# A two-layer graph kernel: which share of the source rows is copied as table columns by ScalarE and VectorE, and which is gathered by GpSimd

## The chip, the cores and the metric

The kernel runs on one core of a Trainium2 chip. Its time is the device time of one execution in microseconds (us). Three runs took 4564.47 us in the median, 4559.45 at the lowest and 4566.27 at the highest. One further execution was profiled. The engines are called as the profile calls them: PE (TensorE, with PEld for its weight loads), DVE (VectorE), ACT (ScalarE), POOL (GpSimd) and SP (SyncE, which only issues DMAs here).

## The reference, cut to what matters

The graph has N = 12500 nodes with 128 features each, and E = 200000 edges, sorted by destination. Two message-passing layers are computed.

```
h     = max(layernorm(x), 0)
feat  = relu(h @ W_pool + b_pool)
neigh = segment_max(feat[src] * w, dst)             # layer 1: a maximum per node
h1    = relu(normalize(h @ W1_self + neigh @ W1_neigh + b1))
agg   = segment_sum(h1[src] * w, dst) / deg         # layer 2: a sum per node
out   = x + relu(h1 @ W2_self + agg @ W2_neigh + b2)
```

What costs time is the reading of `feat[src]` and `h1[src]`: for each of the 200000 edges, and in each layer, one row of 128 floats at a place that only the data knows.

## The kernel before

**Groups and chunks.** The edges are taken in 391 groups of 512, and a group in four chunks of 128 edges (the last group has three chunks). A chunk's source rows land as a tile of 128 edges by 128 features in a buffer of the group. A chunk is filled in one of two ways.

**A gather** is one indirect DMA that POOL issues (`gather`, L581): 128 rows of 512 bytes are read from the table in DRAM (`feat_d` in layer 1, `h_d` in layer 2). POOL does nothing else in the main loops but issue gathers and wait for buffers.

**A column chunk** (class `Columns`) doesn't touch DRAM for its rows. Beside the table in DRAM there is a transposed table in SBUF (`one_way` in layer 1, `other_way` in layer 2), in which a node is one column over 128 partitions. The list of a chunk's 128 column addresses is loaded by SP (`load`), read 16 at a time into registers (`places_of`, L803), and then ACT copies one column per instruction (`one_by_one`, L849) or DVE two columns per instruction (`two_by_two`, L865). That makes 128 ACT or 64 DVE instructions for a chunk. Eight bursts of 16 columns (`fetch`) are planned over the turns before the group is due. After them the chunk has to be turned: in layer 1 by a product with the weights (`multiplied`, L1019 and L1020) and an ACT pass (`cut`, L1023), in layer 2 by a transpose on PE (`turned`, L1213) and an ACT copy back (`back`).

**Which groups.** `every` and `first` say which groups have a column chunk. In layer 1 DVE has one in each 6th group from group 32 on, ACT one in each 5.5th from 28 on. In layer 2 DVE has one in each 3rd from 17 on, ACT one in each 3.5th from 12 on. That is 126 column chunks in layer 1 and 228 in layer 2. `gather` leaves out the chunk that a `Columns` object takes.

**Turns.** Each layer is one Python loop whose turns are written out in order; each engine runs its instructions in that order. In layer 1, turn i issues the gathers of group i, transposes group i on PE (`pm`, L1102), scans group i-1 on DVE with the running maximum (L1117), picks, transposes and places the results of the groups before (`sc`, `pr` L1157, `rows` L1112, `pn` L1166, window copy L1051), and now and then finishes a tile of nodes (`nodes1`). In layer 2, turn i issues the gathers of group i, makes the group's weighted place matrix on DVE (`place` L1227, `s` L1231), multiplies group i-1 on PE (`pa`, L1239), and adds the product of group i-2 to the sums on DVE (L1242).

**How far POOL runs ahead.** POOL's queue holds gathers alone, so POOL is ahead of the other engines until a buffer is missing. In layer 1 the number of buffers falls as the sums fill the memory they are lent from: 38 up to group 75, then 20, 16, 12 and 8 (`ROOM`, `ring_at`). In layer 2 there are 16. `follow` adds waits: from group 60 on in layer 1, and in all of layer 2, a gather of group i also waits for what `mark` noted in an earlier turn (i minus `lag_of(i)`, or i minus 10): PE's transposes in layer 1, and in both layers each eighth ACT column copy of that turn.

```
made = nc.gpsimd.indirect_dma_start(out=gt[:k, j, :], ...)
if behind is not None:
    follow(made, g - behind, n / len(left))
```

The functions that the diff touches, and what calls them, with the line numbers of the profile:

Of the kernel before, what the change touches and what calls it, by code (L numbers as in the profile page):

```python
# [45 lines left out]
CATCH = 9  # L46
# [9 lines left out]
def gnn_kernel(ctx, tc, x, src, dst, ew, w_pool, b_pool, w1s, w1n, b1, w2s, w2n, b2, out):  # L56
# [14 lines left out]
    N = x.shape[0]  # L71
# [5 lines left out]
    NG = GF + 1  # L77
# [587 lines left out]
    for i in range(len(groups) + 4):  # L665
# [59 lines left out]
        while raw_chunks and i <= 15:  # L725
            r, j = raw_chunks[0]
# [8 lines left out]
        k = i - len(groups)  # L735
# [33 lines left out]

    class Columns:  # L770

        def __init__(self, engine, copy, ahead_of, table, layer, lists, slot, after, lead, j, every, first, end):
            self.engine, self.copy, self.ahead_of = engine, copy, ahead_of
            self.table, self.layer, self.at = table.bitcast(U8), layer, TABLES_AT[layer]
            self.lists, self.slot, self.j = lists, slot, j
            self.place, self.held, self.plan = {}, {}, {}
            self.order, self.ready, self.pending = [], set(), None
            while (g := first + int(len(self.place) * every)) < end:
                self.place[g] = len(self.place) % 2
                begin = g - int(every) - lead  # L780
                steps = P // BURST
                assert begin >= 3
                for turn, step in ((begin - 2, self.load), *((g + k, step) for k, step in after)):
                    self.plan.setdefault(turn, []).append((step, g, 0))
                for k in range(steps):
                    turn = begin + int(k * every / steps)
                    self.plan.setdefault(turn, []).append((self.fetch, g, k * BURST))
                    self.order.append((g, k * BURST, turn))

# [55 lines left out]
    def lists_of(k):  # L845
        return [listed[at:at + 1, :] for at in (64 * k, 64 * k + 32)]

    def by_scalar(out, in_, **scale):
        return nc.scalar.activation(out, in_, AF.Copy, **scale)  # L849
# [141 lines left out]
    with tc.manual_schedule(), tc.tile_pool(name="ew", bufs=3) as wk, \  # L991
# [12 lines left out]
        pms, scs, sels, prs, rws, pas = ({} for _ in range(6))  # L1004
        products = {}
        bycol = []
        for k, engine, copy, j, every, first in (
                (0, mybir.EngineType.DVE, two_by_two, 1, 6, 32),
                (1, mybir.EngineType.Activation, one_by_one, 3, 5.5, 28)):
# [12 lines left out]
            def cut(g, _, k=k, rows_of_chunk=rows_of_chunk):  # L1022
                nc.scalar.activation(rows_of_chunk(g), products.pop((g, k)), AF.Relu,  # L1023
                                     **({} if k else {"scale": signs}))

            bycol.append(Columns(engine, copy, k == 0, one_way, 0, lists_of(k), slot,
                                 ((-2, multiplied), (-1, cut)), 2, j, every, first, NG - 1))
            bycol[k].multiplied, bycol[k].cut = multiplied, cut
        turn = turns(wide1, 6)
        busy = {}  # L1030
# [11 lines left out]
        def due(k):  # L1042

            return i - k if 0 <= i - k < NG else None
# [24 lines left out]
        end = NG - 1  # L1069
        for i in range(max(turn) + 6):  # L1070
# [35 lines left out]
            g = due(3)  # L1106
# [6 lines left out]
            g = due(1)  # L1113
# [38 lines left out]
            g = due(2)  # L1152
# [7 lines left out]
            g = due(4)  # L1160
# [33 lines left out]
    with tc.manual_schedule(), tc.tile_pool(name="ew2", bufs=3) as wk, \  # L1194
# [7 lines left out]
        nc.vector.memset(nothing, 0.0)  # L1202

        bycol = []
        for k, engine, copy, j, every, first in (
                (0, mybir.EngineType.DVE, two_by_two, 1, 3, 17),
                (1, mybir.EngineType.Activation, one_by_one, 2, 3.5, 12)):

            def slot(g, j=j):
                return buffer(g, False)[:, j, :]  # L1210

            def turned(g, _, k=k, slot=slot):
                nc.tensor.transpose(flip[:, k], slot(g), ident)  # L1213

            def back(g, _, k=k, slot=slot):
                by_scalar(slot(g), flip[:, k], **({} if k else {"scale": signs}))

            bycol.append(Columns(engine, copy, None, other_way, 1, lists_of(k), slot,
                                 ((-2, turned), (0, back)), 3, j, every, first, NG - CATCH))
# [55 lines left out]
        turn = turns(wide2, 3, 2 * EARLY * (Q + 6))  # L1275
# [3 lines left out]
        for i in range(max(turn) + 2):  # L1279
# [19 lines left out]
            g = i - 1  # L1299
# [10 lines left out]
            g = i - 2  # L1310
# [29 lines left out]
    with tc.If(flag > 0):  # L1340
        with tc.tile_pool(name="gt", bufs=1) as tp, tc.tile_pool(name="gw", bufs=2) as wk, \
# [79 lines left out]
def build(inputs):  # L1421
    import numpy as np
    import concourse.bacc as bacc

    nc = bacc.Bacc("TRN2", target_bir_lowering=False, num_devices=1)
    arrays, args = {}, []
    for name in _INS:
        a = np.ascontiguousarray(inputs[name])
        arrays[f"in_{name}"] = a
        args.append(nc.dram_tensor(f"in_{name}", a.shape, mybir.dt.from_np(a.dtype),  # L1430
                                   kind="ExternalInput").ap())
    args.append(nc.dram_tensor("out", inputs["x"].shape, F32, kind="ExternalOutput").ap())
    with tile.TileContext(nc) as tc:
        gnn_kernel(tc, *args)
    return nc, arrays
# [7 lines left out]
```

## Time and profile before

| | us |
|---|---|
| median of three runs | 4564.47 |
| the profiled execution, its own time | 4560.5 |
| its span, first to last instruction | 4558.6 |
| busy PE / PEld | 2224.7 / 1911.2 |
| busy DVE | 3150.7 |
| busy ACT | 2829.6 |
| busy POOL | 2620.6 |

Busy is the time in which an engine had an instruction in execution; the shares of the span are an average over a preparation (up to about 160 us), layer 1 (up to about 2370 us) and layer 2. A row of the groups reads: line, engine, operation, what is written from what, shape, count, then busy us, the mean ns of one, and the idle time just before them with what ended it. "issue" means that the profile shows nothing that the engine waited for, "remote" a semaphore whose sender the profile doesn't name. A row of the windows gives, for a stretch of the span, each engine's busy us and in brackets its number of instructions.

### The profile page before, as it was taken

What the parts mean: (1) busy time and instruction counts of PE and PEld (TensorE: products, weight loads), DVE (VectorE), ACT (ScalarE), POOL (GpSimd) and SP (SyncE); (2) the same over time, 40 slices, a digit from 0 to 9 for tenths busy, and PEclk for the clock granted to TensorE, in tenths of its full rate; (3) what the DMA queues carried; (4) which work ended last, traced back from release to release, by engine and by line L of the source; (5) the groups of instructions that cost most, each with busy time, mean ns of one, the idle gap of its engine ahead of it and who ended that gap; (6) DMA issues with size and microseconds to landing.
All of it is one profiled execution on the core that took longest, in us unless ns stands there. A gap on an engine that the chain in (4) does not pass through costs nothing.

```text
span 4558.6 us, 71416 instructions
## 1 busy us (share of the span) xinstructions
PE 2224.7 (49%) x9505; PEld 1911.2 (42%) x9505; DVE 3150.7 (69%) x16224; ACT 2829.6 (62%) x23893; POOL 2620.6 (57%) x2789
## 2 busy tenths in 40 slices
PE   5525654545555555554443545444444444444445
PEld 3314544444444444444442444344334434434444
DVE  4437987778878777877772667666666666666663
ACT  3425755566666655655543777777777777777773
POOL 5556266665665666566656555555555555555554
PEclk7555555555555555555555555555555555555555
DMA  5313233332332323333321112111111111111111
GB/s 159 101 54 103 77 98 95 96 93 93 96 93 91 96 88 95 92 94 95 94 83 44 41 44 57 48 46 48 49 45 48 47 48 46 48 49 47 49 49 41
DMA packets 136652, 328.01 MB, mean 72 GB/s; under 512 B 50865, under 2 KB 59538, under 8 KB 136164
## 3 DMA queue, kind: packets, MB, share of 16 engines
q0 software_dynamic: 88704, 181.75, 15.7%
q1 hardware_dynamic: 45652, 140.69, 8.6%
q14 instruction: 408, 3.34, 0.2%
q8 instruction: 80, 1.31, 0.1%
q10 hardware_dynamic: 1808, 0.92, 0.1%
HBM read 300.80 MB, written 22.39 MB: 71 GB/s over the span
## 4 chain that ended last, share of the span: by engine, by line
ACT 51%; issue 27%; PE 7%; another core or an unknown queue 5%; DVE 4%; ACTq 4%; DMA 0%; DVEq 0%; POOL 0%; POOLq 0%; SPq 0%
ACT gt L849 25%; ACT ewT L849 7%; ACT way L849 5%; ACTq L803 4%; ACT lastT L849 4%; ACT invT L849 4%; ACT rows L1112 1%; PE pn L1166 1%; PE pr L1157 1%; ACT way L1051 1%; PE pa L1239 1%; DVE pm L1117 1%; PE pf L682 1%; PE pm L1102 1%
## 5 line engine op out<-in xcount | busy, mean ns | idle before, releaser
L849 ACT ACTIVATE gt<-way 128x1 f32 x12032 | 1309.0, 190 | 633.4 <-issue 620.3
L581 POOL DMA_INDIRECT gt<-feat_d,srcT x777 | 733.2, 944 | 570.9 <-issue 176.6
L581 POOL DMA_INDIRECT gt<-h_d,srcT x669 | 631.8, 944 | 449.8 <-issue 122.5
L1157 PE MATMUL pr<-ident,sc 128*128 128x128 f32 x782 | 257.6, 432 | 1025.2 <-ACT rows L1112 635.9
L581 POOL DMA_INDIRECT way<-feat_d,srcT x547 | 517.4, 946 | 338.4 <-issue 122.6
L865 DVE SCALAR_TENSOR_TENSOR gt<-b,way 128x2 f32<-128x2 f32 x3968 | 572.3, 217 | 129.0 <-issue 119.9
L1117 DVE TENSOR_TENSOR_SCAN pm<-kt,pm 128x512 f32<-128x512 f32 x389 | 500.6, 1287 | 153.5 <-remote 91.7
L1157 PEld LDWEIGHTS pr<-ident,sc 128*128 128x128 f32 x782 | 125.5, 206 | 1127.0 <-ACT rows L1112 693.5
L1239 PE MATMUL pa<-s,gt 128*128 128x24 f32 x1566 | 384.0, 390 | 393.6 <-ACT gt L849 223.3
L865 DVE SCALAR_TENSOR_TENSOR picked<-b,way 128x2 f32<-128x2 f32 x3840 | 542.9, 217 | 14.7 <-issue 13.8
L1239 PEld LDWEIGHTS pa<-s,gt 128*128 128x128 f32 x1566 | 353.3, 325 | 423.1 <-ACT gt L849 228.0
L849 ACT ACTIVATE ewT<-way 128x1 f32 x3456 | 370.2, 189 | 139.9 <-issue 136.5
L581 POOL DMA_INDIRECT ewT<-h_d,srcT x327 | 308.5, 943 | 220.4 <-ACT gt L849 108.6
L849 ACT ACTIVATE way<-way 128x1 f32 x2816 | 311.7, 193 | 187.7 <-issue 185.9
L1166 PEld LDWEIGHTS pn<-sel,rows 128*128 128x128 f32 x1564 | 369.8, 325 | 15.7 <-DVE r L934 8.9
L1242 DVE TENSOR_TENSOR way<-pa,way 128x48 f32 x391 | 80.0, 205 | 410.7 <-PE pa L1239 191.0
L1166 PE MATMUL pn<-sel,rows 128*128 128x48 f32 x1564 | 355.3, 375 | 9.8 <-DVE r L934 7.6
L865 DVE SCALAR_TENSOR_TENSOR ewT<-b,way 128x2 f32<-128x2 f32 x1920 | 276.7, 217 | 65.5 <-issue 62.4
L1139 DVE COPY sc<-pm 128x256 f32<-128x256 f32 x391 | 165.3, 423 | 224.3 <-PE pr L1157 113.4
L849 ACT ACTIVATE lastT<-way 128x1 f32 x1920 | 208.0, 189 | 133.0 <-issue 131.2
L1239 PE MATMUL pa<-s,ewT 128*128 128x24 f32 x768 | 188.6, 390 | 204.0 <-ACT ewT L849 104.0
L1239 PEld LDWEIGHTS pa<-s,ewT 128*128 128x128 f32 x768 | 173.5, 325 | 228.5 <-ACT ewT L849 106.2
(352 smaller groups left out, 5032.5 us busy)
## 6 DMA issues: line engine op xcount, KB each, us to landing
kt<-ratio_d SPq DMA_DIRECT2D x129, 768.0 KB
gt<-feat_d,srcT POOLq DMA_INDIRECT x777
gt<-h_d,srcT POOLq DMA_INDIRECT x669
way<-feat_d,srcT POOLq DMA_INDIRECT x547
feat_d<-fr SPq DMA_DIRECT2D x24, 256.0 KB
xr<-in_x SPq DMA_DIRECT2D x24, 256.0 KB
out<-o SPq DMA_DIRECT2D x24, 256.0 KB
h_d<-h SPq DMA_DIRECT2D x47, 128.0 KB
```

The lines of the kernel that those rows point to most:

```text
L581: made = nc.gpsimd.indirect_dma_start(out=gt[:k, j, :], out_offset=None, in_=table_d[:, :], in_offset=bass.IndirectOffsetOnAxis(ap=places, ...
L682: nc.tensor.matmul(pf[:, q, :], rows[:, q, :], W["pool"], start=False, stop=q == n - 1)
L803: _, self.held[g, r] = nc.values_load_multi_w_load_instructions(self.lists[self.place[g]][:, r:r + BURST], [self.engine], min_val=self.at, ...
L849: return nc.scalar.activation(out, in_, AF.Copy, **scale)
L865: nc.vector.scalar_tensor_tensor(slot[:, r + e:r + e + 2], zero_high, columns_read[e], columns_read[e + 1].to_broadcast([P, 2]), op0=OP.su ...
L1051: nc.scalar.activation(agg1[:, bass.ds(at, LW)], pas.pop(g), AF.Copy)
L1117: nc.vector.tensor_tensor_scan(pm[:, :ne], kt[:, :ne], pm[:, :ne], carry, op0=OP.mult, op1=OP.max)
L1139: nc.vector.tensor_copy(sc[:, :ne // 2], two[:, :, 0])
L1157: nc.tensor.transpose(prs[g][:k, j, :], sc[:, j * P:j * P + k], ident)
L1166: nc.tensor.matmul(pas[g], rows[:k, j, :], sel[:k, j, :], start=j == 0, stop=j == len(chunks) - 1)
L1239: nc.tensor.matmul(pas[g][:, SHIFT[j]:SHIFT[j] + CW], gt[:k, j, :], s[:k, j, :], start=False, stop=j == 0)
L1242: nc.vector.tensor_tensor(agg2[:, bass.ds(at, LW)], pas.pop(g), agg2[:, bass.ds(at, LW)], OP.add)
```

## The change

`Columns` gets one more parameter, `spread`: the turns over which the eight bursts of a chunk are laid out, which was `every` so far. In layer 1 the first group of both `Columns` objects becomes N = 12500, which lies beyond the last group, so that no chunk of layer 1 is a column chunk. In layer 2 DVE has one in each 14th group from 22 on and ACT one in each 13th from 20 on, that is 26 and 28 chunks, with their bursts spread over 11 turns. A gather by POOL takes the place of each column chunk that is gone: 126 in layer 1 and 174 in layer 2.

```diff
-        def __init__(self, engine, copy, ahead_of, table, layer, lists, slot, after, lead, j, every, first, end):
+        def __init__(self, engine, copy, ahead_of, table, layer, lists, slot, after, lead, j, every, spread, first, end):
...
             while (g := first + int(len(self.place) * every)) < end:
                 self.place[g] = len(self.place) % 2
-                begin = g - int(every) - lead
+                begin = g - int(spread) - lead
...
                 for k in range(steps):
-                    turn = begin + int(k * every / steps)
+                    turn = begin + int(k * spread / steps)
...
-                (0, mybir.EngineType.DVE, two_by_two, 1, 6, 32),
-                (1, mybir.EngineType.Activation, one_by_one, 3, 5.5, 28)):
+                (0, mybir.EngineType.DVE, two_by_two, 1, 6, 6, N),
+                (1, mybir.EngineType.Activation, one_by_one, 3, 5.5, 5.5, N)):
...
-                                 ((-2, multiplied), (-1, cut)), 2, j, every, first, NG - 1))
+                                 ((-2, multiplied), (-1, cut)), 2, j, every, spread, first, NG - 1))
...
-                (0, mybir.EngineType.DVE, two_by_two, 1, 3, 17),
-                (1, mybir.EngineType.Activation, one_by_one, 2, 3.5, 12)):
+                (0, mybir.EngineType.DVE, two_by_two, 1, 14, 11, 22),
+                (1, mybir.EngineType.Activation, one_by_one, 2, 13, 11, 20)):
...
-                                 ((-2, turned), (0, back)), 3, j, every, first, NG - CATCH))
+                                 ((-2, turned), (0, back)), 3, j, every, spread, first, NG - CATCH))
```

More of the change, by code (lines that the diff above doesn't have):

```diff
@@ L1006, in gnn_kernel @@
         bycol = []
-        for k, engine, copy, j, every, first in (
-                (0, mybir.EngineType.DVE, two_by_two, 1, 6, 32),
-                (1, mybir.EngineType.Activation, one_by_one, 3, 5.5, 28)):
+        for k, engine, copy, j, every, spread, first in (
+                (0, mybir.EngineType.DVE, two_by_two, 1, 6, 6, N),
+                (1, mybir.EngineType.Activation, one_by_one, 3, 5.5, 5.5, N)):
             def rows_of_chunk(g, j=j):
@@ L1204, in gnn_kernel @@
         bycol = []
-        for k, engine, copy, j, every, first in (
-                (0, mybir.EngineType.DVE, two_by_two, 1, 3, 17),
-                (1, mybir.EngineType.Activation, one_by_one, 2, 3.5, 12)):
+        for k, engine, copy, j, every, spread, first in (
+                (0, mybir.EngineType.DVE, two_by_two, 1, 14, 11, 22),
+                (1, mybir.EngineType.Activation, one_by_one, 2, 13, 11, 20)):
             def slot(g, j=j):
```

## The prediction

> **What bounds the kernel now.** I read the page first, its busy line and its chain of waits.
>
> ```profile
> span 4558.6 us, 71416 instructions
> ...
> PE 2224.7 (49%) x9505; PEld 1911.2 (42%) x9505; DVE 3150.7 (69%) x16224; ACT 2829.6 (62%) x23893; POOL 2620.6 (57%) x2789
> ...
> ACT 51%; issue 27%; PE 7%; another core or an unknown queue 5%; DVE 4%; ACTq 4%; DMA 0%; DVEq 0%; POOL 0%; POOLq 0%; SPq 0%
> ...
> L849 ACT ACTIVATE gt<-way 128x1 f32 x12032 | 1309.0, 190 | 633.4 <-issue 620.3
> ```
>
> ACT's column copies hold the chain, and POOL is busy for 57% only. Read alone, this says: take the copies from ACT and give them to the idle POOL. But 27% of the chain is "issue", time in which ACT waited for nothing that the profile shows, and the copies' row has 620 us of it. So the next question is when ACT is held up. The timelines of POOL and of ACT at the start of layer 2 answer it.
>
> ```profile
> 2450.32 0.94 POOL L581 DMA_INDIRECT gt<-h_d,srcT  x1 [0.30 <-issue]
> 2451.56 0.94 POOL L581 DMA_INDIRECT gt<-h_d,srcT  x1 [0.30 <-issue]
> 2456.98 0.94 POOL L581 DMA_INDIRECT gt<-h_d,srcT  x1 [4.47 <-remote]
> 2463.98 0.94 POOL L581 DMA_INDIRECT gt<-h_d,srcT  x1 [6.06 <-remote]
> ```
>
> ```profile
> 2449.70 0.20 ACT L849 ACTIVATE lastT<-way 128x1 f32 x1 [1.20 <-issue]
> ...
> 2462.30 0.20 ACT L849 ACTIVATE lastT<-way 128x1 f32 x1 [0.50 <-issue]
> 2463.00 0.20 ACT L849 ACTIVATE lastT<-way 128x1 f32 x1 [0.50 <-issue]
> 2463.70 1.59 ACT L849 ACTIVATE lastT<-way 128x1 f32 x16 [0.50 <-issue]
> ```
>
> While POOL issues gathers without a pause (0.94 us and a gap of 0.30, so one in 1.248 us), one ACT copy comes every 0.7 to 1.4 us. From 2463.70 on, 16 copies take 1.59 us, ten times faster. The slow state outlasts the run of gathers: after 2451.56 only one more comes, at 2456.98, and ACT is still slow 6 us behind that one. So something shared is behind with work that the gathers left. Not only ACT suffers. The scans of layer 1 and the window adds of layer 2 count the turns (groups of four windows, 161.3 to 281.1, 310 to 372, 600 to 2200, and 2383 to 2452.5):
>
> ```profile
> L1117 DVE TENSOR_TENSOR_SCAN pm<-kt,pm x5: 1284/1287/1289, 174.5 to 272.4; 128x512 f32<-128x512 f32 x5
> L1117 DVE TENSOR_TENSOR_SCAN pm<-r_f,pm x2: 1222/1254/1287, 164.9 to 169.6; 128x512 f32<-128x512 f32 x2
> ```
>
> ```profile
> L1117 DVE TENSOR_TENSOR_SCAN pm<-kt,pm 128x512 f32<-128x512 f32 x12 | 15.4, 1286 | 2.3 <-ACT pm L1089 2.3
> ```
>
> ```profile
> L1117 DVE TENSOR_TENSOR_SCAN pm<-kt,pm 128x512 f32<-128x512 f32 x291 | 375.0, 1289 | 127.7 <-remote 77.2 <-PE pm L1102 32.9 <-PE pn L1166 7.1
> ```
>
> ```profile
> L1242 DVE TENSOR_TENSOR way<-pa,way 128x48 f32 x3 | 0.6, 209 | 53.3 <-remote 48.4 <-PE pa L1239 4.9
> ```
>
> ```profile
> 161.30:281.10 119.80, 25.40 (x66) 14.14 (x65) 31.45 (x112) 22.19 (x56) 90.57 (x96) 0.53 0.26 72
> ```
>
> Under continuous gathers (the last row is the windows' one for the first run, with POOL's 96 gathers in its last bracket) a turn takes 17 us (7 scans in 120 us) and 23 us (3 adds in 69.5 us); otherwise 5.2 us (62 / 12) and 5.5 us (1600 / 291). So POOL's 57% is not free time: when POOL fills it, the others starve.
>
> **What a gather costs.** In the windows, the count of POOL and of all other engines together gives the mean interval of gathers, and how many instructions were served beside each.
>
> ```profile
> core 0: us, PE busy (x) PEld busy (x) DVE busy (x) ACT busy (x) POOL busy (x), PEclk, DMA share, GB/s
> 161.30:301.70 140.40, 25.40 (x66) 14.14 (x65) 31.45 (x112) 24.41 (x61) 95.29 (x101) 0.53 0.23 64
> 310.00:372.00 62.00, 39.51 (x151) 26.18 (x151) 42.11 (x144) 31.04 (x89) 37.06 (x41) 0.68 0.26 80
> 600.00:2200.00 1600.00, 828.45 (x3657) 715.84 (x3656) 1261.27 (x5064) 964.23 (x7792) 962.82 (x1020) 0.53 0.31 94
> 2368.00:2463.90 95.90, 23.89 (x98) 21.19 (x99) 21.93 (x50) 18.30 (x102) 65.25 (x68) 0.50 0.22 57
> 2600.00:4400.00 1800.00, 837.31 (x3531) 738.93 (x3531) 1209.63 (x8119) 1307.65 (x12109) 1040.36 (x1103) 0.50 0.18 48
> ```
>
> The first and fourth row run from the first gather of a long run to where the others move again:
>
> ```profile
> 161.36 0.94 POOL L581 DMA_INDIRECT way<-feat_d,srcT  x1 [34.44 <-DMA feat_d<-fr]
> ```
>
> ```profile
> 301.76 0.60 ACT L622 ACTIVATE ewT<-pn 128x512 f32<-128x512 f32 x1 [6.94 <-remote]
> ```
>
> ```profile
> 2368.08 1.03 POOL L581 DMA_INDIRECT er<-h_d,srcT  x1 [15.97 <-DVE r L934]
> ```
>
> Starved run 1: 140.4 us / 101 gathers = 1.390, with 304 / 101 = 3.0 other instructions per gather. Starved run 2: 95.6 / 68 = 1.406, with 5.1. Raw stage (310 to 372, no column copies, four gathers a group): 62 / 41 = 1.512, with 13.0. Layer 1: 1600 / 1020 = 1.569, with 19.8. Layer 2: 1800 / 1103 = 1.632, with 24.7. The five lie on a line. From the mean of the first two (4.1; 1.398) to the last, the slope is 0.234 / 20.7 = 0.0113 us per instruction and the start 1.352 us; the line gives 1.500 for the raw stage and 1.576 for layer 1, within 0.012 of what was measured. I read it as one shared path on which a gather takes about 1.35 us and another engine's instruction about 0.011 us, and which is full in all five stages. What the path is, the trace doesn't say. On this reading the kernel is bound by the sum of both, and ACT's "issue" is its queue for the path.
>
> **The change part by part.** Against the profiled execution's 4560.5 us (span 4558.6 and 1.9 around it), which is 4 us under the median; 0.2%, some 9 us, is what a measurement can tell from no change.
>
> *Layer 1 up to group 75.* POOL waits here for buffers, with the longest wait of the span:
>
> ```profile
> 550.24 0.94 POOL L581 DMA_INDIRECT gt<-feat_d,srcT  x1 [70.19 <-PE pm L1102]
> ```
>
> ```profile
> L865 DVE SCALAR_TENSOR_TENSOR picked<-b,way 128x2 f32<-128x2 f32 x384 | 54.2, 217 | 2.9 <-issue 2.8
> ```
>
> The second row is from 390 to 560 us: DVE's column copies are 54.2 of 170 us, and they go. The wait can end earlier, by at most the 70 us less the 17 more gathers before it (17 x 1.248 = 21): 49. Bounds 0 to -49; I take the middle, -25.
>
> *Layer 1 from there on.* 550.24 to 2351.2 us, 1801 us, with 1150 gathers (last brackets of the windows below, ahead of the rows where layer 1's gathers end and layer 2's begin and end); 109 column chunks of these groups (52 on DVE, 57 on ACT) become gathers, so 1259.
>
> ```profile
> 540.00:2352.00 1812.00, 930.84 (x4136) 805.81 (x4136) 1427.97 (x5740) 1083.89 (x8766) 1085.76 (x1150) 0.54 0.31 94
> 2383.70:4521.00 2137.30, 972.70 (x4105) 859.81 (x4105) 1377.14 (x9147) 1493.64 (x13794) 1249.00 (x1323) 0.50 0.18 48
> ```
>
> ```profile
> 2351.21 0.90 POOL L581 DMA_INDIRECT gt<-feat_d,srcT  x1 [0.30 <-PE pm L1102]
> ```
>
> ```profile
> 2383.73 0.96 POOL L581 DMA_INDIRECT gt<-h_d,srcT  x1 [0.30 <-issue]
> ```
>
> ```profile
> 4519.99 0.90 POOL L581 DMA_INDIRECT gt<-h_d,srcT  x1 [0.30 <-issue]
> ```
>
> Other instructions per group now: 20169 / 291 = 69.3. Away go 128 / 5.5 = 23.3 on ACT, 64 / 6 = 10.7 on DVE, and 7 per chunk for the bias, product and cut, 2.4. That leaves 32.9 a group or 8.2 a gather, and 1.352 + 8.2 x 0.0113 = 1.445. The raw stage, which is the nearest in kind (four gathers a group, no copies), lay 0.0125 over the line, so I take 1.4575. 1259 x 1.4575 = 1835: **+34 us**. Bounds from rows: 1.398 (nothing but gathers) and 1.512 (the raw stage).
>
> *Layer 2.* 1323 gathers from 2383.7 to 4520.0 take 2136 us; 174 more make 1497, 3.86 a group. The adds between 2600 and 4400 us count the groups:
>
> ```profile
> L1242 DVE TENSOR_TENSOR way<-pa,way 128x48 f32 x328 | 67.0, 204 | 267.5 <-PE pa L1239 154.8 <-PE pn L920 56.2 <-issue 20.0
> ```
>
> Other instructions: 27290 in 1800 us, 328 groups, 83.2 a group. Away go 36.6 (ACT), 21.3 (DVE) and 1.9 (turning); 9.85, 4.6 and 0.4 come back for one chunk in 13 and one in 14. That leaves 38.3 a group, 9.9 a gather: 1.464. 1497 x 1.464 = 2191: **+55 us**. The same bounds.
>
> *Costed at nothing.* 300 of the 354 list loads on SP (0.5 KB each) go; SP's other work stays. In layer 2 a column burst now starts 14 turns ahead into a buffer whose last reader, the product of the group 16 before, was issued one turn earlier; DVE stands in this wait ahead of its place matrix and its add. The add waits for that same product anyway; if not covered, 26 chunks times one fast turn (5.5 us at most) is below 143 us, and below nothing it can't be. Fewer turns carry ACT marks, so fewer gathers wait for ACT; what is late next is PE's transposes (layer 1) and products (layer 2), about 25 PE and PEld instructions a group (3657 + 3656 over 291).
>
> Sum: 4558.6 - 25 + 34 + 55 = 4622.6, and 1.9 around it: **4625 us**, 1.4% over the profiled execution. At one interval for both layers the change breaks even where 2756 gathers take 4558.6 - 596 us: at 1.438 us.
>
> **The rivals.** *POOL's own pace decides* (faster): the other engines, without their copies, keep up beside continuous gathers. Then 1.248 us holds: 1259 x 1.248 = 1571 (-230), 1497 x 1.248 = 1868 (-268), -25: 4038 us. For it: 96 gathers in a row did hold this pace. Against it: turns of 17 and 23 us in those runs, without ACT copies in the first. Chance 0.10. The Trainium skill (page "Runtime: NRT & Kernel Launch", section "Instruction fetch mechanics") has instruction fetch run by itself ahead of dispatch, which is slower, so that it stays hidden in straight code; by that rule ACT would not be held up and this rival would win. The trace disagrees where it shows ACT copies with 1.20 us of "issue" before each.
>
> *The path carries the gathers alone* (slightly faster): the other instructions cost nothing once they are few. 1.398 in both layers: 1760 (-41), 2093 (-43), -25: 4451 us. For it: the two starved runs. Against it: there the others got no more than a turn in 17 us. It decides below 1.438. Chance 0.16.
>
> *PE is late for each group* (slower): PE's 25 instructions a group come through only while POOL pauses, so that each group needs a pause, as in the raw stage. 1.512 in both: 1904 (+103), 2264 (+127), and no gain early: 4790 us. For it: the raw stage had no copies either. Against it: its turns had a product and four norms more. Chance 0.20.
>
> **How the numbers follow.** 0.54 is left for the forecast, whose own range I put at 4560 to 4700. The range over all reaches from the second to the third rival, 4450 to 4790, and leaves out the first. Faster by over 0.2%: 0.10 and 0.16 of the rivals, 0.01 of the forecast's lower end, 0.27. Within 0.2%: 0.08, out of the forecast. Slower: 0.65.
>
> **What would show it.** In the windows after: gathers 1.44 to 1.48 us apart in both layers, not 1.25; DVE and ACT far below now, and no engine near full; POOL's pauses ended by PE; PE idle with "issue" before it in runs of gathers; POOL ahead by all its buffers. If the runs of gathers are long and turns stay under 5 us, the shared path is wrong. If the interval is above 1.5 with few instructions, PE's lateness is the price and not the path.

## The result and the profile after

The changed kernel takes 4696.2 us (median of four runs, 4674.4 to 4703.7), the kernel before 4563.8 (4559.5 to 4566.3). The ratio is **1.0283**, 95% interval 1.0245 to 1.0322: 132 us slower. The forecast had the direction and the mechanism's sign, but not the size: 4625, 61 us above this median of before. The profiled execution took 4689.1 us.

The page of the changed kernel: its span, its busy line, and its chain of waits by engine.

```profile
span 4687.3 us, 38451 instructions
...
PE 1977.2 (42%) x8953; PEld 1751.4 (37%) x8953; DVE 1763.9 (38%) x6240; ACT 889.7 (19%) x5161; POOL 2902.7 (62%) x3089
...
another core or an unknown queue 25%; PE 10%; DVE 5%; issue 4%; DVEq 1%; ACT 0%; POOL 0%; DMA 0%; ACTq 0%; POOLq 0%
```

The program has little more than half as many instructions, no engine is busy for more than 62%, and it is slower. ScalarE, 51% of the chain before, is gone from it; what is left of the chain lies mostly with a releaser that the profile doesn't name. (The shares add up to 45% only, so over half of the span isn't on this chain.) Its windows from the first to the last gather of layer 1 behind group 75, and of layer 2 (they reach 1 us past the last gather's start), and the two gathers that begin them:

```profile
535.70:2376.70 1841.00, 745.35 (x3774) 682.40 (x3773) 946.55 (x2215) 246.47 (x1026) 1188.37 (x1259) 0.58 0.31 95
2408.80:4647.80 2239.00, 923.97 (x3928) 829.97 (x3929) 505.29 (x2998) 475.21 (x3638) 1413.09 (x1497) 0.50 0.19 50
```

```profile
535.75 0.94 POOL L581 DMA_INDIRECT gt<-feat_d,srcT  x1 [49.62 <-PE pm L1102]
...
2408.88 0.96 POOL L581 DMA_INDIRECT gt<-h_d,srcT  x1 [0.31 <-issue]
```

| Term | Forecast | Measured |
|---|---|---|
| start of layer 1 (wait ends at 550.24 before) | -25 | -14.5 |
| layer 1, 1259 gathers | 1835 us, 1.4575 each | 1840 us, 1.462 each |
| layer 2, 1497 gathers | 2191 us, 1.464 each | 2238 us, 1.495 each |

The gathers were counted right (1259, 1497), and so were the instructions beside them: 3774 + 3773 + 2215 + 1026 over 1259 is 8.6 in layer 1 (8.2 forecast), 14493 over 1497 is 9.7 in layer 2 (9.9). Layer 1 came out as worked. Of the 64 us between 4625 and 4689, **47 are layer 2's interval**, 10 the start, 5 layer 1, and the rest the seam and the tail. So the experiments ask first what layer 2 has that layer 1 has not. GpSimd's waits between 2600 and 4400 us (in total, times, the longest; a row for each buffer's name) give a first hint: those for ScalarE are few and long. The rows with "issue", left out here, are the gap of 0.30 us between two gathers.

```profile
...
POOL gt L581 <- remote: 74.3, 39, 3.9
POOL gt L581 <- ACT ewT L849: 51.4, 8, 12.3
POOL gt L581 <- ACT gt L849: 43.2, 10, 10.1
...
POOL ewT L581 <- ACT lastT L849: 26.5, 3, 13.9
...
POOL gt L581 <- PE pa L1239: 9.1, 18, 3.9
```

### The profile page after: what moved, and what is told of

Same layout as the page of the kernel before. It is cut to its first block, busy times and chain, and to the rows that moved or that the text cites. A ratio compares the mean times of both kernels' runs of the same rounds, so it can differ in the third digit from the quotient of the medians.

```text
span 4687.3 us, 38451 instructions
## 1 busy us (share of the span) xinstructions
PE 1977.2 (42%) x8953; PEld 1751.4 (37%) x8953; DVE 1763.9 (38%) x6240; ACT 889.7 (19%) x5161; POOL 2902.7 (62%) x3089
## 3 DMA queue, kind: packets, MB, share of 16 engines
q8 instruction: 76, 1.25, 0.1%
## 5 line engine op out<-in xcount | busy, mean ns | idle before, releaser
L581 POOL DMA_INDIRECT gt<-feat_d,srcT x859 | 810.9, 944 | 503.7 <-issue 195.4
L581 POOL DMA_INDIRECT gt<-h_d,srcT x755 | 713.0, 944 | 424.6 <-issue 198.1
L1239 PEld LDWEIGHTS pa<-s,gt 128*128 128x128 f32 x1566 | 349.5, 327 | 389.2 <-DVE s L1231 175.0
L1112 ACT ACTIVATE rows<-pr 128x256 f32<-128x256 f32 x392 | 150.1, 383 | 1542.1 <-remote 1178.7
L1239 PE MATMUL pa<-s,gt 128*128 128x24 f32 x1566 | 372.3, 389 | 131.2 <-issue 54.9
L849 ACT ACTIVATE gt<-way 128x1 f32 x1792 | 232.7, 192 | 762.1 <-issue 426.2
L1237 PE MATMUL pa<-nothing,ones_r 1*128 1x48 bf16 x391 | 82.0, 210 | 606.5 <-DVE way L1242 380.2
L1239 PEld LDWEIGHTS pa<-s,ewT 128*128 128x128 f32 x768 | 171.8, 327 | 255.4 <-DVE s L1231 163.6
L920 PE MATMUL pn<-w_2n,way 128*128 128x128 f32 x192 | 74.1, 488 | 420.1 <-DVE way L1242 302.0
L581 POOL DMA_INDIRECT lastT<-h_d,srcT x186 | 175.5, 944 | 109.2 <-issue 46.6
L1129 DVE TENSOR_SCALAR sel<-cols,lastT,invT 128x48 f32<-128x48 f32 x782 | 238.5, 305 | 0.0
L581 POOL DMA_INDIRECT invT<-h_d,srcT x185 | 174.5, 943 | 91.3 <-issue 44.4
L920 PEld LDWEIGHTS pn<-w_2n,way 128*128 128x128 f32 x192 | 52.9, 323 | 436.8 <-DVE way L1242 312.0
```

What stands on the lines that cost most here:

```text
L581: made = nc.gpsimd.indirect_dma_start(out=gt[:k, j, :], out_offset=None, in_=table_d[:, :], in_offset=bass.IndirectOffsetOnAxis(ap=places, ...
L920: nc.tensor.matmul(po, nT, W[neigh_w], start=False, stop=True)
L1112: nc.scalar.activation(rws[g][:k, j, :], pr[:k, j, :], AF.Copy)
L1129: nc.vector.tensor_scalar(part, cols[:k, 1, :], lastT[:k, t, j, r:r + 1], invT[:k, t, j, r:r + 1], op0=OP.is_equal, op1=OP.mult)
L1237: nc.tensor.matmul(pas[g], ones_r[0:1, :P], nothing[0:1, :], start=True, stop=False)
L1239: nc.tensor.matmul(pas[g][:, SHIFT[j]:SHIFT[j] + CW], gt[:k, j, :], s[:k, j, :], start=False, stop=j == 0)
```

## The experiments

The runs came to be on chips of two kinds, which nothing in the kernels decides: on two chips the kernel before takes 4507 and 4508 us, close to the chip of the prediction, and on four others 3496 to 3499. A ratio is always against the kernel before on the same chip. The interval of gathers in layer 1 and layer 2 is a window's length over its gathers, and the rows of the windows have the columns of the prediction (PE, PEld, DVE, ACT, POOL). Four runs that repeat a kernel on the second kind of chip are told of below the table.

| Run | Before, us | Ratio and 95% interval | Layer 1 | Layer 2 |
|---|---|---|---|---|
| layer 1 changed alone | 4507 | 1.0077 (1.0060 to 1.0093) | 1.450 | 1.598 |
| layer 2 changed alone | 4507 | 1.0260 (1.0232 to 1.0288) | 1.552 | 1.485 |
| no columns at all | 4507 | 1.0262 (1.0244 to 1.0279) | 1.449 | 1.418 |
| changed, short spread | 4507 | 1.0255 (1.0238 to 1.0273) | 1.448 | 1.458 |
| half rows, 16 + 16 copies | 4508 | 1.0581 (1.0550 to 1.0612) | 1.448 | 1.484 |
| changed | 3499 | 1.1062 (1.1043 to 1.1080) | 1.249 | 1.248 |
| no columns, 32 copies on ScalarE | 3497 | 1.4210 (1.4186 to 1.4233) | 1.249 | 1.248 |
| no columns, 32 copies on VectorE | 3497 | 1.3339 (1.3317 to 1.3361) | 1.249 | 1.629 |
| no columns, 16 + 16 copies | 3499 | 1.1302 (1.1283 to 1.1321) | 1.249 | 1.249 |
| no columns, memset of 64 | 3497 | 1.1429 (1.1410 to 1.1448) | 1.249 | 1.287 |
| no columns, memset of 224 | 3499 | 1.2017 (1.1997 to 1.2037) | 1.249 | 1.420 |
| no columns, half rows | 3499 | 1.1060 (1.1037 to 1.1082) | 1.249 | 1.205 |
| before, columns by 4.5 in layer 1 | 3498 | 0.9951 (0.9938 to 0.9965) | 1.249 | 1.249 |
| the same, by 2.75 in layer 2 | 3496 | 1.0302 (1.0288 to 1.0316) | 1.251 | 1.343 |

### The layers apart, and the spread

Four kernels on one chip. The first two take the change for one layer each:

```diff
 # layer 1 alone: layer 2 as before
-                (0, mybir.EngineType.DVE, two_by_two, 1, 14, 11, 22),
-                (1, mybir.EngineType.Activation, one_by_one, 2, 13, 11, 20)):
+                (0, mybir.EngineType.DVE, two_by_two, 1, 3, 3, 17),
+                (1, mybir.EngineType.Activation, one_by_one, 2, 3.5, 3.5, 12)):
 # layer 2 alone: layer 1 as before
-                (0, mybir.EngineType.DVE, two_by_two, 1, 6, 6, N),
-                (1, mybir.EngineType.Activation, one_by_one, 3, 5.5, 5.5, N)):
+                (0, mybir.EngineType.DVE, two_by_two, 1, 6, 6, 32),
+                (1, mybir.EngineType.Activation, one_by_one, 3, 5.5, 5.5, 28)):
```

> Layer 1 of the changed kernel (no columns), layer 2 of the kernel before. In the changed kernel layer 1 gained 14.5 us up to group 76 and lost 39 behind it. Shared path (a gather about 1.35 us, another instruction 0.0113): layer 2's interval depends on its own instructions alone, so +25 us, about 4588, with layer 2 at 1.61 to 1.63 us per gather. If layer 1's long runs leave something behind for layer 2, more than that.

> Layer 1 of the kernel before, layer 2 of the changed kernel. Shared path and every other theory in which the layers don't touch each other: layer 2's loss alone, 2238 - 2136 = +102 us, about 4666. With the first run of this set the two should add up to the +132 us of the whole change.

The third has no columns in layer 2 either (a first group of N is never reached), the fourth spreads a chunk's copies over 3 and 3.5 turns and keeps all else of the change:

```diff
 # no columns at all
+                (0, mybir.EngineType.DVE, two_by_two, 1, 14, 11, N),
+                (1, mybir.EngineType.Activation, one_by_one, 2, 13, 11, N)):
 # short spread
+                (0, mybir.EngineType.DVE, two_by_two, 1, 14, 3, 22),
+                (1, mybir.EngineType.Activation, one_by_one, 2, 13, 3.5, 20)):
```

> The changed kernel without columns in layer 2 too: 54 more gathers, 1551 in layer 2. Shared path: 23.4 other instructions a group, 5.85 a gather, 1.352 + 5.85 x 0.0113 = 1.418, so 2199 us, 39 less than the changed kernel's 2238: 4657. Shared path with layer 2's excess of 0.031 us that nothing explains yet: 1.449, 2247, +9: 4705. The few column chunks that are left come late and hold the turns: without them 1.418 or less, 4657 or below. Long runs of gathers starve whatever else there is, and set 1.495 by themselves: 2319, +81: 4777.

> The changed kernel, a chunk's copies spread over 3 and 3.5 turns as before, not over 11; as many columns and gathers. Shared path: the same instructions per gather, so the same time, 4696 within 15 us. The spread is what makes it worse (copies that begin 14 turns ahead wait for a buffer, and their marks tie nearly every gather to ScalarE): the interval falls from 1.495 to the forecast 1.464, 46 us less, 4650. Copies in a bunch come later still when others starve: more than 4715.

The windows of layer 1 and layer 2 of the first:

```profile
534.60:2360.30 1825.70, 728.77 (x3784) 672.44 (x3784) 947.64 (x2221) 246.38 (x1029) 1192.42 (x1259) 0.59 0.30 96
2390.90:4505.40 2114.50, 973.93 (x4120) 862.70 (x4121) 1377.09 (x9148) 1491.84 (x13796) 1252.22 (x1323) 0.50 0.17 48
```

of the second:

```profile
539.70:2324.90 1785.20, 920.64 (x4109) 797.42 (x4108) 1415.03 (x5702) 1080.43 (x8724) 1085.32 (x1150) 0.54 0.29 95
2356.70:4580.30 2223.60, 920.47 (x3914) 826.52 (x3914) 507.23 (x3001) 472.71 (x3638) 1413.08 (x1497) 0.50 0.17 50
```

and of layer 2 in the third and in the fourth:

```profile
2384.50:4584.40 2199.90, 905.26 (x3860) 820.64 (x3860) 299.08 (x1337) 0.00 (x0) 1463.88 (x1551) 0.50 0.18 52
```

```profile
2387.40:4570.50 2183.10, 924.28 (x3928) 833.52 (x3929) 546.60 (x2998) 445.52 (x3638) 1416.43 (x1497) 0.50 0.18 51
```

Both layers lose: 35 us by layer 1, 117 by layer 2 (25 and 102 expected from the first chip). Whether the two add up wasn't seen, as the changed kernel itself didn't run on this chip. Take the first kernel's two rows and draw the prediction's line through them: layer 1 has 8.6 other instructions per gather and 1.450 us, layer 2 has 23.6 and 1.598, so 0.0099 us per instruction and 1.365 for a gather (0.0113 and 1.352 in the prediction; the expectations have 0.0087, since they put 20.8 instructions between layer 2 with and without columns, where the windows count 17.7). This line gives 1.560 for the second kernel's layer 1 (19.7; measured 1.552), 1.423 for no columns (5.8; 1.418) and 1.461 for the short spread (9.7; 1.458). The one row that it misses is the second kernel's layer 2, with the 11-turn spread: 1.461 by the line, **1.485** measured. The second and the fourth kernel have the same 1497 gathers and 14467 against 14493 other instructions there, and differ by 2223.6 - 2183.1 = **40.5 us**. So the spread costs some 40 us, and that is most of the 47 that the forecast lacked.

Where it goes, the waits of GpSimd between 2600 and 4400 us tell (waits in total, times, the longest). The four largest that ScalarE ended, with the long spread and with the short one:

```profile
POOL gt L581 <- ACT gt L849: 48.5, 12, 9.6
POOL gt L581 <- ACT ewT L849: 47.6, 7, 10.5
...
POOL invT L581 <- ACT gt L849: 18.5, 3, 8.7
POOL ewT L581 <- ACT lastT L849: 17.3, 3, 6.3
```

```profile
POOL ewT L581 <- ACT gt L849: 27.2, 15, 6.4
POOL invT L581 <- ACT ewT L849: 19.9, 6, 8.7
POOL gt L581 <- ACT invT L849: 17.2, 9, 6.3
POOL gt L581 <- ACT gt L849: 16.1, 6, 6.6
```

132 us against 80, and 166 against 102 over all that ScalarE ended. A gather waits for the copies that ScalarE made ten turns earlier, if there were any in that turn. By the planner's rule a chunk's eight bursts lie in 8 of 13 turns with the long spread and in 4 with the short one; before, every turn had some. So it isn't the number of such turns that grew with the change. The timelines of ScalarE and of GpSimd in the second kernel show what the copies wait for:

```profile
3478.57 3.18 ACT L849 ACTIVATE ewT<-way 128x1 f32 x32 [29.56 <-PE pa L1239]
```

```profile
3468.23 0.94 POOL L581 DMA_INDIRECT gt<-h_d,srcT  x1 [0.30 <-issue]
3479.69 0.94 POOL L581 DMA_INDIRECT gt<-h_d,srcT  x1 [10.51 <-ACT ewT L849]
```

A chunk that begins 14 turns ahead writes into a buffer that PE's product (L1239) has yet to read. ScalarE's first copies wait for this product, and 1.1 us after they start, when the marked copy is done, the gather goes on. Of GpSimd's 28 waits of more than 1 us that ScalarE ended in this window, 27 (161 us) ended within 3 us of ScalarE's own going on after a wait of more than 4 us: in 16 for that product, in 11 for a releaser that the profile doesn't name. With the short spread a chunk begins 6 turns ahead, and that holds for 10 of 29, in 3 for that product. The waits thus point at the two together: the early start, which makes ScalarE wait for PE, and the marks, which hand this wait on to GpSimd. A kernel with the long spread and no marks, or with the long spread and a later start into a free buffer, was not run, so the trace alone says this and no experiment separates them.

### The price on the other chips

Then the price of an instruction was to be measured by itself, on the kernel without columns: constant copies on one engine, a slower pace of GpSimd, and gathers of half the rows.

```diff
 # 32 on ScalarE (the first copy alone) or on VectorE (the second alone)
+            for _ in range(32):
+                nc.scalar.activation(spare2[:, 0:1], spare[:, 0:1], AF.Copy)
+                nc.vector.tensor_copy(spare2[:, 0:1], spare[:, 0:1])
 # 16 on each
+            for _ in range(16):
+                nc.scalar.activation(spare2[:, 0:1], spare[:, 0:1], AF.Copy)
+                nc.vector.tensor_copy(spare2[:, 2:3], spare[:, 1:2])
 # slower pace: behind each gather, spare of 64 or 224 columns
+                nc.gpsimd.memset(spare, 0.0)
 # half rows
+            k = min(k, rows)    # rows is 64 in layer 2, 128 in layer 1
```

> The kernel without columns in both layers (ratio 1.0262, 1.4186 us per gather in layer 2), with 32 copies of one constant column into a spare tile on ScalarE in each turn of layer 2, 8 per gather; they read and write nothing that anything waits for. Shared path with a price per instruction: the first four runs put it at 0.0087 us (1.4186 to 1.5987 over 20.8 instructions), so +0.070, 1.489, +108 us, ratio 1.050; by the forecast's 0.0113, +0.090, ratio 1.057. ScalarE is on no chain of layer 2 without columns: if only an engine that others wait for costs anything, 1.42 and 1.026.

> The same with the 32 copies on VectorE, on which each turn hangs (place matrix and window add). Shared path: the same price whatever the engine, +0.070 to +0.090, ratio 1.050 to 1.057. Lateness: in a run of gathers VectorE gets one instruction in 0.7 to 1.4 us, so 32 more in each turn hold the turn, and each needs a pause: 32 x 0.1 us in the pause at the least, 0.8 us a gather, +1200 us, ratio above 1.25.

> The kernel without columns in both layers, with a memset of 128 x 64 on GpSimd behind each gather of layer 2, so that its gathers come some 0.1 to 0.2 us further apart than 1.249. Shared path: POOL's pauses shrink by as much, and the interval stays at 1.42 (1.43 with the memset's own instruction): ratio 1.026 to 1.030. Pauses are a latency that each run pays, whatever the pace in it: +0.1 to +0.2 a gather, +155 to +310 us, ratio 1.06 to 1.095. Runs without a gap are what starves the others: they keep up now, and the interval is POOL's own, 1.35 to 1.40, ratio 1.00 to 1.02.

> The kernel without columns in both layers; each gather of layer 2 fetches the first 64 of its 128 rows, the other rows are left out. Path by gathers: 1.42 as before, ratio 1.026. Path by rows: 0.68 + 5.85 x 0.0087 = 0.73 and then POOL's own time decides, which is unknown for 64 rows, between 0.62 and 1.25: interval 0.75 to 1.25, layer 2 shorter by 260 to 1040 us, ratio 0.80 to 0.97.

On this chip the kernel before takes 3497 us. The windows of both layers with the 32 copies on ScalarE and the group of these copies, then the windows of layer 2 with 32 on VectorE and with the memset of 64:

```profile
348.30:1971.00 1622.70, 929.76 (x3752) 720.42 (x3752) 942.36 (x2204) 246.97 (x1017) 1226.94 (x1299) 0.52 0.35 109
1988.00:3924.20 1936.20, 915.17 (x3979) 838.87 (x3980) 311.66 (x1373) 1674.77 (x8259) 1463.61 (x1551) 0.50 0.22 60
```

```profile
L1326 ACT ACTIVATE spare<-spare 128x1 f32<-128x1 f32 x12704 | 2576.3, 203 | 403.5 <-DVE spare L1204 1.4
```

```profile
1985.30:4512.00 2526.70, 909.04 (x3831) 815.48 (x3831) 2079.24 (x13319) 0.00 (x0) 1463.06 (x1551) 0.50 0.17 46
```

```profile
1986.20:3982.30 1996.10, 914.87 (x3979) 838.65 (x3980) 311.46 (x1373) 0.00 (x0) 1731.93 (x3102) 0.50 0.22 58
```

Gathers come 1.249 apart in this window of layer 1 and 1.248 in layer 2 beside ScalarE's copies: GpSimd hardly ever waits, and the others keep up. All four expectations were made for the first kind of chip and say nothing here. What the runs do show: 32 copies were too many for either engine (ScalarE has done 8259 of its 12704 when the gathers end, so that the kernel takes 4970; VectorE is busy for 82% of a layer 2 that has grown to 2527). With the memset the interval is 1.287, GpSimd's own pace. Half of the rows took 1.205 (ratio 1.1067).

So the next set had room on both engines, and the changed kernel itself beside it.

> The kernel without columns in both layers, with 16 copies of a constant column on ScalarE and 16 on VectorE in each turn of layer 2, 8 more instructions per gather, as in the two runs with 32, but with room on both engines (16 x 0.234 = 3.7 us of a turn of 5 us). On a chip where before takes some 4500 us: by a price of 0.0087 us per instruction the interval goes from 1.4186 to 1.489, ratio 1.050; if static copies cost the path nothing, 1.42 and 1.026. On a chip where before takes 3500 us and gathers come 1.249 apart: no price is to be seen, 1.249.

> The kernel without columns in both layers, with a memset of 128 x 224 on GpSimd behind each gather of layer 2: some 0.17 us more than with 128 x 64, which made 1.28, so one gather in about 1.45. On a chip where before takes some 4500 us, shared path: the other engines are served in the gaps, POOL's pauses go, and the interval is POOL's own, 1.43 to 1.46, ratio 1.03 to 1.04. If each stretch of gathers needs a pause whatever its pace: 1.45 + 0.17 = 1.62, ratio 1.095. On a chip where before takes 3500 us: 1.45 by POOL alone, ratio 1.21.

> The changed kernel as it is, beside the others. On a chip where before takes some 4500 us: ratio 1.028 to 1.034, as measured first. On a chip where before takes 3500 us, where gathers come 1.249 apart in every stage: 300 more gathers are 300 x 1.249 = 375 us, ratio 1.107, and GpSimd's own pace decides in both kernels.

> The kernel without columns in both layers; each gather of layer 2 fetches 64 of its 128 rows, the other rows are left out. On the chip where before took 3497 us it took 1.205 a gather against 1.249: GpSimd's time is nearly all per gather. On a chip where before takes some 4500 us: if the path's price is per gather, 1.42 again, ratio 1.026; if it is per row (1.36 / 128 = 0.0106 us, close to the 0.0087 of an instruction), 0.68 + 5.85 x 0.0087 = 0.73, below GpSimd's 1.205, so 1.205 decides: layer 2 331 us shorter, ratio 0.95.

Again a chip where the kernel before takes 3499. The changed kernel's two layers and its busy line, and layer 2 with 16 + 16 copies:

```profile
349.20:1970.40 1621.20, 929.83 (x3752) 720.88 (x3752) 942.37 (x2204) 247.02 (x1019) 1225.77 (x1298) 0.52 0.35 109
1987.60:3856.60 1869.00, 927.49 (x4033) 844.47 (x4034) 518.32 (x3037) 368.37 (x3638) 1412.92 (x1497) 0.50 0.22 60
```

```profile
PE 2137.9 (55%) x8953; PEld 1780.4 (46%) x8953; DVE 1768.0 (46%) x6240; ACT 785.1 (20%) x5161; POOL 2904.0 (75%) x3089
```

```profile
1986.80:3923.60 1936.80, 915.17 (x3980) 838.78 (x3981) 1233.06 (x7629) 1287.95 (x6351) 1464.23 (x1551) 0.50 0.23 60
```

Here the whole change is one product: 300 more gathers by 1.249 is 375 us, and 3870.6 - 3498.9 = 372 was measured. Eight more instructions per gather leave the interval at 1.249: no price at all. With the memset of 224 it is 1.420 (1.45 was expected), with half rows 1.205, GpSimd's own in each case. The 16 + 16 copies and the half rows were run once more, on a third chip of this kind, with the same outcome (ratios 1.1302 and 1.1077):

> No columns in both layers, 16 constant copies on ScalarE and 16 on VectorE in each turn of layer 2. Where before takes some 4500 us: a price of 0.0087 us for any instruction gives 1.4186 + 8 x 0.0087 = 1.489 per gather, ratio 1.050; if only instructions that others wait for cost anything, 1.42 and 1.026; if the price is that of copies from an address in a register, 1.42 too. Where before takes some 3500 us: 1.249, ratio 1.130, as measured.

> No columns in both layers, 64 of 128 rows per gather in layer 2, the other rows left out. Where before takes some 4500 us: price by call, 1.42, ratio 1.026; price by row, 0.73, so that GpSimd's own 1.205 decides, ratio 0.95; part by part, between the two. Where before takes some 3500 us: 1.205, ratio 1.106, as measured.

The last two runs of that kernel have both edits in one, half rows and 16 + 16 copies. The first fell on a chip where the kernel before takes 3496 us (1.205 per gather, ratio 1.1115, as expected), the second on one where it takes 4508:

> No columns in both layers, 64 of 128 rows per gather in layer 2 (the others left out), and 16 constant copies each on ScalarE and VectorE per turn of layer 2. Where before takes some 4500 us: price by call and by instruction, 1.489 per gather, ratio 1.050; by call, with constant copies free, 1.42 and 1.026; by row, 0.68 + 13.85 x 0.0087 = 0.80, so that GpSimd's own 1.205 decides, ratio 0.95. Where before takes some 3500 us: 1.205, layer 2 in 1870 us, ratio 1.11.

> No columns in both layers, 64 of 128 rows per gather in layer 2 (the others left out), 16 constant copies each on ScalarE and VectorE per turn of layer 2. Where before takes some 4500 us: price by call and by instruction, 1.489 per gather, ratio 1.050; by call, with constant copies free, 1.42 and 1.026; by row, 0.80, so that GpSimd's own 1.205 decides, ratio 0.95. Where before takes some 3500 us: 1.205, ratio 1.11, as measured before.

The same program's layer 2, there:

```profile
2386.00:4688.30 2302.30, 913.42 (x3847) 819.46 (x3847) 1163.73 (x7343) 1286.77 (x6345) 1395.25 (x1551) 0.50 0.11 28
```

1.484 per gather, against 1.489 expected for a price by call and by instruction (1.418 + 8 x 0.0087), 1.42 for copies that cost nothing, and 1.205 for a price by row. By division that is 0.066 / 8 = **0.0083 us** for a constant copy, and half of the rows give nothing back. It is one run with two edits: that a saving by rows was hidden by dearer copies isn't excluded. Nor is it a price of copies for which nothing waits. Nothing reads them, but VectorE's 16 stand in its queue ahead of the next place matrix, and PE waits for that: between 2600 and 4400 us PE ended 155 us of GpSimd's waits here and 24 without columns, and VectorE's share of the chain is 41% against 9%. The chain of this run, and a row of the waits of PE's weight loads (PEld):

```profile
DVE 41%; another core or an unknown queue 27%; issue 16%; PE 11%; ACT 3%; POOL 1%; DVEq 0%; DMA 0%; ACTq 0%; POOLq 0%
...
PEld pa L1245 <- DVE spare L1330: 185.1, 36, 13.5
```

So later turns may make up the 0.066 as well as a price on a shared path. A kernel with 16 copies a turn on ScalarE alone would tell the two apart; it was not run on this kind of chip. (The ratio, 1.058 against 1.050, is higher for VectorE's copies: 334 of them, 51 us of the last 83, are still to be done when the gathers have ended.) ScalarE in this kernel, on a chip where before takes 3496 us, and where it takes 4508:

```profile
2999.80 10.29 ACT L1329 ACTIVATE spare<-spare 128x1 f32<-128x1 f32 x44
```

```profile
3013.02 8.18 ACT L1329 ACTIVATE spare<-spare 128x1 f32<-128x1 f32 x35 [0.50 <-ACT spare L1329]
...
3022.93 0.20 ACT L1329 ACTIVATE spare<-spare 128x1 f32<-128x1 f32 x1 [0.76 <-ACT spare L1329]
3022.93 0.15 DVE L1330 COPY spare<-spare 128x1 f32<-128x1 f32 x1 [0.55 <-DVE spare L1330]
3023.63 0.20 ACT L1329 ACTIVATE spare<-spare 128x1 f32<-128x1 f32 x1 [0.50 <-ACT spare L1329]
3023.64 0.15 DVE L1330 COPY spare<-spare 128x1 f32<-128x1 f32 x1 [0.55 <-DVE spare L1330]
3024.33 0.20 ACT L1329 ACTIVATE spare<-spare 128x1 f32<-128x1 f32 x1 [0.50 <-ACT spare L1329]
3024.34 0.15 DVE L1330 COPY spare<-spare 128x1 f32<-128x1 f32 x1 [0.55 <-issue]
```

44 copies in 10.29 us, 0.234 each, on the one; on the other the same pace at first (35 in 8.18 us), and some 8 us into the run of gathers a copy each 0.70 us, VectorE's at the same instants as ScalarE's. The copies read and write fixed columns of two spare tiles, each engine its own columns, so neither an address in a register nor another engine's data can hold them.

### The other way: fewer gathers

On either kind of chip a gather that is saved is worth more than an instruction. So the kernel before with more columns, in layer 1 on ScalarE, and then in layer 2 on VectorE too:

```diff
-                (1, mybir.EngineType.Activation, one_by_one, 3, 5.5, 5.5, 28)):
+                (1, mybir.EngineType.Activation, one_by_one, 3, 4.5, 4.5, 28)):
 # the second kernel, beside it
-                (0, mybir.EngineType.DVE, two_by_two, 1, 3, 3, 17),
+                (0, mybir.EngineType.DVE, two_by_two, 1, 2.75, 2.75, 17),
```

> The other way: the kernel before, with ScalarE's columns of layer 1 in each group by 4.5 instead of 5.5, 15 gathers fewer. Where before takes some 3500 us and gathers set the pace: 15 x 1.249 = 19 us less, ratio 0.995; ScalarE is then busy for 4.0 of 4.5 us in a turn of layer 1, and if that is too tight, 1.00 to 1.01. Where before takes some 4500 us: a chunk takes 128 copies, 8 register loads and some 3 more, 139 x 0.0087 = 1.21 us, against 1.36 for its gather: 2 us less, ratio 1.000.

> The kernel with ScalarE's columns by 4.5 groups in layer 1 (ratio 0.9951), and VectorE's columns in layer 2 in each group by 2.75 instead of 3, 11 gathers fewer again. Where before takes some 3500 us: 11 x 1.249 = 14 us less, 32 us in all, ratio 0.991; VectorE is then busy for 91% of layer 2 (85% and 11 chunks of 64 copies of 0.141 us in 1650 us), and if that is too tight, 0.995 or above. Where before takes some 4500 us: a chunk of VectorE has 64 copies and about 11 more instructions, 75 x 0.0087 = 0.65 us, against 1.36 for its gather: 8 us less and 2 of layer 1, ratio 0.998.

Layer 1 and layer 2 of the first, and layer 2 of the second:

```profile
416.40:1795.60 1379.20, 962.39 (x4098) 800.59 (x4097) 1358.25 (x5568) 1138.13 (x10225) 1042.20 (x1104) 0.53 0.38 119
1812.60:3465.40 1652.80, 1008.32 (x4207) 873.54 (x4208) 1371.08 (x9181) 1396.70 (x13796) 1249.67 (x1323) 0.50 0.23 62
```

```profile
1814.10:3576.00 1761.90, 1000.92 (x4163) 864.52 (x4163) 1469.05 (x9870) 1403.87 (x13807) 1239.26 (x1312) 0.50 0.21 58
```

The first takes 3481.7 us, **0.9951** of before there (0.9938 to 0.9965): 15 gathers by 1.249 is 19 us, 17 were measured. It beats both kernels on a chip of this kind; on the other kind it was not run. There is little more to be had of this in layer 1, where VectorE is now busy for 1358 of 1379 us. The second lost it again and more (1.0302, where 0.991 was expected). Layer 2 has 11 gathers fewer and is 109 us longer, with VectorE busy for 83% only. In the planner's rule a chunk's eight bursts lie 3, 3 and 2 to a turn; three turns apart chunks don't meet, but by 2.75 each fourth begins two turns after the last, and that turn has 5 bursts. That it is this crowding, and not the lead that is a turn shorter, was not shown.

## Why the prediction was right, and where it was wrong

**The shared path** held on the kind of chip that it was read from. Five stages of before gave 1.352 and 0.0113 us; another chip gave 1.365 and 0.0099, and these two met three more stages there within 0.008. The second rival (gathers alone, 1.398 in both layers) is out by layer 1's 1.462, and by 1.458 with 9.7 other instructions against 1.418 with 5.8 on one chip. The third (1.512 in both layers, set by PE) is out by layer 1's 1.462 and by 1.418 without columns. But the line is a fit: whether the other instructions take turns on one path with the gathers, or come late in runs of gathers and so make GpSimd wait, no run separates.

**Layer 1** (1.4575 forecast, 1.462 measured) was right. The line alone with the measured 8.6 instructions gives 1.449; the 0.0125 taken over from the raw stage made up the rest, and as no run shows what it stands for, that it fits is in part luck. **The start** was taken from the middle of two bounds, -25 of 0 to -49, and came to -14.5: the wait shrank from 70.19 to 49.62 us.

**Layer 2** was wrong, and the step that failed is the one under "costed at nothing". There the wait of a burst that begins 14 turns ahead, into a buffer whose last reader was issued one turn earlier, was put at nothing, with a bound of 143 us, and looked at for VectorE alone. The next sentence said that fewer gathers wait for ScalarE, and that PE is what is late next. Fewer did wait: between 2600 and 4400 us ScalarE ended 311 of GpSimd's waits before (370.9 us, none over 4.0) and 47 after. But these 47 still took 184.6 us, up to 13.9, against 35.3 for PE's and 137.8 without a named releaser. So ScalarE stayed what is late, now because its copies wait for the buffer, and the marks hand that wait to GpSimd. The spread cost 40.5 us in the like comparison, less than the bound; how much of it is the buffer and how much the marks stays open. The term of instructions was right: with the short spread, the same instructions come to 1.458 on a chip where the line gives 1.461. The sign "POOL's pauses ended by PE" failed with the step, and 1.495 lies over the 1.44 to 1.48 that was named.

**The first rival**, GpSimd's own pace, has the right mechanism on four other chips: 1.249, with no hold-up. Its time there was still wrong in sign, since it set that pace for the changed kernel alone. Where the others keep up, the kernel before has that pace as well (1.249 in both layers with the columns by 4.5), and 300 more gathers cost 372 us. No chip ran the change faster. The Trainium skill (page "Runtime: NRT & Kernel Launch", section "Instruction fetch mechanics") holds that instruction fetch stays hidden in straight code. The second kind of chip agrees (a constant copy in 0.234 us beside gathers without a pause). On the first a copy came each 0.70 us, but whether it is fetch that is late there, no run shows, so the prediction's "the trace disagrees" said too much (and of the copies that it shows, one has 1.20 us of "issue" before it and three have 0.50).

**What the argument could not see:** the prices were read from one trace as if the kernel had them. They belong to the kernel on a kind of chip: on the other kind the same instructions cost GpSimd nothing.

## What to carry to other kernels

An engine that is idle by its busy share isn't free: measure what one more of its instructions takes from the others where it runs without a pause, and compare that price (here 1.36 us or 1.25 us for a gather) with what the work costs where it is (64 or 128 copies of 0.01 us). When work is thinned out but begun earlier, ask what its first instruction then waits for, and who waits for that instruction in turn; a wait on an idle engine counts as soon as another engine is tied to it. A price that is read from one trace may be that of one chip, so repeat the kernel before on another before building on it.

## What the runs showed of the hardware

Two kinds of chip: the same program takes 4507 to 4564 us on what ran here of the first kind and 3496 to 3499 on four of the second, with the same granted clock in layer 2 (0.50 in each of the windows shown). On the first kind, some 8 us into a run of gathers, ScalarE and VectorE came down to a copy each 0.70 us, both at the same instants; on the second kind's stretch shown there is nothing of it. What differs between the chips, the traces don't say.

A gather's time on GpSimd hardly depends on its rows: 1.205 us apart with 64, 1.249 with 128. And part of the gap behind it is free: a memset of 0.17 us between two gathers made them 1.28 apart, since the gap shrank from 0.30 to 0.16 us, as GpSimd's timeline in that kernel has it.

```profile
2600.04 0.18 POOL L588 MEMSET spare<- 128x64 f32 x1
2600.38 0.95 POOL L582 DMA_INDIRECT ewT<-h_d,srcT  x1 [0.16 <-issue]
2601.33 0.17 POOL L588 MEMSET spare<- 128x64 f32 x1
2601.66 0.95 POOL L582 DMA_INDIRECT ewT<-h_d,srcT  x1 [0.16 <-issue]
```
